# Two chunks' maps as four quarter products in a four-layer graph network

## The chip, the cores and the metric

The kernel runs on one core of one Trainium2 chip. The metric is the device time of one launch in microseconds, lower is better; a kernel's time is the median of its runs. Beside the timed runs there is one profiled execution, from which every duration below comes.

## The reference, cut to what matters

Eight graphs share 2048 nodes with 64 features each. Four layers follow one another, each a LayerNorm, a ReLU, a graph layer and a residual. The change touches layer 2, which takes three steps of the same recurrence:

```python
def _L2_gnn_ref(causal_vars, adj_matrix, intervention_value, W1, b1, W2, b2, intervention_idx):
    v = causal_vars.at[:, intervention_idx].set(intervention_value)
    for _ in range(MAX_STEPS):                       # 3
        effects = jnp.einsum('nm,bmd->bnd', adj_matrix, v)
        h = jnp.concatenate([v, effects], axis=-1)
        h = jax.nn.relu(jnp.einsum('bnk,dk->bnd', h, W1) + b1)
        v = jnp.einsum('bnk,dk->bnd', h, W2) + b2
    return v
...
h = jnp.maximum(_layernorm(x, axis=-1), 0.0)
x = x + _L2_gnn_ref(h, adj, L2_gnn_intervention_value, L2_gnn_W1, L2_gnn_b1, L2_gnn_W2, L2_gnn_b2, 0)
```

Layer 3 takes products of the adjacency with the features twice (Chebyshev terms) and applies a weight of each node's own.

## The kernel before, in words

**Layout.** Two graphs make a pair and stand one above the other on the 128 partitions: partitions 0 to 63 hold the features of graph 0 of the pair, 64 to 127 those of graph 1; nodes run along the free dimension. There are 4 pairs (`p`), and 4 chunks (`c`) of 512 nodes in a pair. A weight of 64x64 that acts on features stands twice on the diagonal of a 128x128 matrix (`W1v`, `Wvc`, `Wec`), and half of such a matrix is zero.

**Layer 2.** `W1` is split into the part for `v` and the part for `effects`. The map by `W2` after a step is folded into the weights of the next one: `Wvc` and `Wec` are those folded matrices, `b1c` and `cb` the folded biases. In steps 1 and 2, `v` therefore holds the ReLU of the step before. For each pair and step the kernel has `y`, the features of all 16 node tiles multiplied by the `effects` weights, nodes on partitions, as a high and a low part in fp32r. For each chunk one PSUM accumulator `acc` (two buffers) takes

- one fp32 product of 128x128 by 128x512, `Wvc` (in step 0 `W1v`) times the chunk of `v` (L2081), and then
- in `spread`, for each of the 16 node tiles `m` two fp32r products, the high and the low part of `y` with the adjacency tile `aT[m]` (L1984 to L1991).

ScalarE writes the ReLU of the accumulator back into the chunk of `v` (L2084). After steps 0 and 1, `carry` makes the chunk's part of the next step's `y`: `moved` multiplies the chunk by `Wec` (four products `py`, one for each node tile), VectorE adds the bias (`yb`, L1952), ScalarE casts the high part (L1954) and VectorE takes the low part (L1955). After step 2, `leave` multiplies by `W2` (`pv`), adds the residual, transposes (`tx`), normalizes for layer 3, and transposes back (`tv`).

**What sets the order.** TensorE's order is that of the program. The chains `carry` and `leave` are Python generators, and a `Weave` with a clock of estimated microseconds slips their pieces in among the products: each `spread` tile counts 0.47, the product by `Wvc` 0.93, and a chain that yields `1.4` gives its next piece once the clock has passed 1.4 after its start. The other engines' order comes from the framework's scheduler, each engine executes in order, and a tile whose memory was used before waits for that use.

**Beside it.** In steps 0 and 1, `raw` loads two blocks of the adjacency a chunk on SP's queue into a tag `x` of two buffers, and `check` (L1927) tests on VectorE that they hold only zeros and ones. At the first pair `weights(1)` loads the weights of layer 3 (`W3f`, two halves on SP, L2062) and the embedding, and `weights(2)` changes `W3f` on VectorE (L2066, L2067). Just before layer 2, layer 1 ends with `e` (L1760) on VectorE and a DMA on GpSimd's queue that adds `e` to memory (L1762).

All matmuls of these layers go through one helper, so they carry the line L734 (transposes L741) in the profile; they are told apart by the tile that they write and by their shapes.

Of the kernel before, what the change touches and what calls it, by code (L numbers as in the profile page):

```python
# [8 lines left out]
FP = mybir.dt.float32  # L9
FR = mybir.dt.float32r  # L10
AF = mybir.ActivationFunctionType
# [5 lines left out]
P = 128  # L17
# [3 lines left out]
NT = N // P  # L21
CW = 512
# [5 lines left out]
def half(b2):  # L28
    return slice(b2 * 64, (b2 + 1) * 64)


def cols(c, w=CW):
    return slice(c * w, (c + 1) * w)
# [602 lines left out]
class Kit:  # L636
# [95 lines left out]
    def mm(self, *args, **kw):  # L732

        one = self.nc.tensor.matmul(*args, **kw)  # L734
        if self.strict:
            self.tc.keep_in_program_order(one)
# [1162 lines left out]
def layers23(self, aT):  # L1899
    kit, x2_dram, x3_dram, out, ctx, fin, v = (  # L1900
        self.kit, self.x2_dram, self.x3_dram, self.out, self.ctx, self.fin, self.v
    )
    tc, nc, t, mm = kit.tc, kit.nc, kit.t, kit.mm
    W1v, W1e, W2, Wvc, Wec, cb = kit.W1v, kit.W1e, kit.W2, kit.Wvc, kit.Wec, kit.cb
    b1, b2c, ivc, b1c = kit.b1, kit.b2c, kit.ivc, kit.b1c
    K3, D3 = 3, 16
    LAST = NCW - 1
    w2 = ctx.enter_context(tc.tile_pool(name="w2f", bufs=1, reuse_waits="tile"))
    sb = ctx.enter_context(tc.tile_pool(name="f_sb", bufs=2, reuse_waits="tile"))
    ps = ctx.enter_context(tc.tile_pool(name="f_ps", bufs=2, space=PSUM, reuse_waits="tile"))  # L1910
    weave = Weave()
# [26 lines left out]
    LENT = (None, None, ("fold", 2), ("pr", 3))  # L1938

    def moved(v, c, W, bias, lent=None):  # L1940

        py = ps.tile([P, 4, P], FP, tag="tp", name="py")
        for k in range(4):
            m = 4 * c + k
            mm(py[:, k, :], v[:, m * P : (m + 1) * P], W, start=True, stop=True)
        return in_parts(py, bias, lent)

    def in_parts(py, bias=None, lent=None):
        hi, lo = parts(lent)
        if bias is not None:  # L1950
            yb = fin.tile([P, 4, P], FP, tag="ca", name="yb")
            nc.vector.tensor_tensor(yb, py, bias[:, None, :].to_broadcast([P, 4, P]), op=OP.add)  # L1952
            py = yb
        nc.scalar.copy(hi, py)  # L1954
        nc.vector.tensor_tensor(lo, py, hi.bitcast(FP), op=OP.subtract)  # L1955
        return hi, lo
# [27 lines left out]
    def spread(acc, y, c, start, ms):  # L1984

        for m in ms:
            weave.until(lambda: y[m // 4] is not None)
            for h, part in enumerate(y[m // 4]):
                mm(acc, part[:, m % 4, :], aT[m][:, cols(c)], start=start, stop=m == NT - 1 and h == 1)
                start = False  # L1990
            weave.passed(0.47)  # L1991

    def load(dst, src, c):
        nc.sync.dma_start(out=dst, in_=src[:, cols(c)])
        return dst

    def chunk_of(src, c):
        return load(fin.tile([P, CW], FP, tag="x", name="xp"), src, c)
# [8 lines left out]
        y[c] = moved(src, k, W1e, None)  # L2007

    def carry(c, step, yn):
        yield 1.4  # L2010
        yn[c] = moved(v, c, Wec, cb, None if step else LENT[c])

    def leave(p, c, xp, yn):

# [40 lines left out]
    y = self.y  # L2055
    W3 = w2.tile([P, K3, D3 * F], FP, name="W3f")
    emb = w2.tile([P, NT, D3], FP, name="embf")

    def weights(step):
        if step == 1:  # L2060
            for h in range(2):
                nc.sync.dma_start(out=W3[half(h)], in_=t["L3_gnn_weight"])  # L2062
            nc.sync.dma_start(out=emb, in_=t["L3_gnn_embedding"].rearrange("(t p) d -> p t d", p=P))
            return

        nc.vector.tensor_sub(W3[:, 0, :], W3[:, 0, :], W3[:, 2, :])  # L2066
        nc.vector.tensor_scalar(W3[:, 2, :], W3[:, 2, :], 2.0, None, op0=OP.mult)  # L2067

    every = range(NT)
    for p in range(NP):  # L2070
        for step in range(3):
            yn = [None] * NCW
            if p == 0 and step:
                weights(step)
            for c in range(NCW):
                acc = ps.tile([P, CW], FP, tag="acc", name="acc")
                if step < 2:
                    got = raw(2)
                else:
                    xp = chunk_of(x2_dram[p], c)  # L2080
                mm(acc, Wvc if step else W1v, v[:, cols(c)], start=True, stop=False)  # L2081
                weave.passed(0.93)
                spread(acc, y, c, False, every)
                nc.scalar.activation(v[:, cols(c)], acc, AF.Relu, bias=b1c if step else b1)  # L2084
                if step < 2:
                    check(got)
                weave.start(carry(c, step, yn) if step < 2 else leave(p, c, xp, yn))
            y = yn


        y1 = sb.tile([P, N], FP, tag="y1", name="y1", bufs=1)
        yn, after = [None] * NCW, [None] * NCW

        two = [ps.tile([P, CW], FP, tag="acc", name="acc") for c in range(2)]
        for ms in (range(0, 8), range(8, 12), range(12, NT)):
            for c in range(2):
                spread(two[c], y, c, 0 in ms, ms)
                if NT - 1 in ms:
                    nc.scalar.copy(y1[:, cols(c)], two[c])
                    weave.start(again(y1, c, yn))  # L2100
        for c in range(2, NCW):
            acc = ps.tile([P, CW], FP, tag="acc", name="acc")
            spread(acc, y, c, True, every)
            nc.scalar.copy(y1[:, cols(c)], acc)
            weave.start(again(y1, c, yn))
        xn = None
        for c in range(NCW):
            xr = chunk_of(x3_dram[p], c)
            acc = ps.tile([P, CW], FP, tag="acc", name="acc")
            if xn is not None:  # L2110
                weave.start(enter(c - 1, after, xn, 0.2, ("u0", "u1")))
                if c == LAST:
                    weave.start(enter(c, after, xl, 0.6, ("u0", "u1"), y1))
            spread(acc, yn, c, True, every)
            y2 = fin.tile([P, CW], FP, tag="ca", name="y2")
            nc.scalar.copy(y2, acc)
            if c < LAST and p + 1 < NP:
                xn = chunk_of(x2_dram[p + 1], c)
                if c == LAST - 1:
                    xl = load(y1[:, cols(0)], x2_dram[p + 1], LAST)  # L2120
            for k in range(4):
                i = 4 * c + k
                ns, ks = slice(i * P, (i + 1) * P), slice(k * P, (k + 1) * P)
                pr = []
                for w in range(2):
                    u = [ps.tile([P, 8, F], FP, tag=f"u{h}", name=f"u{h}") for h in range(2)]
                    for kk, src in enumerate((v[:, ns], y1[:, ns], y2[:, ks])):
                        for h in range(2):

                            mm(  # L2130
                                u[h].rearrange("p d o -> p (d o)"), src[half(h), :], W3[half(h), kk, cols(w)],
                                start=kk == 0, stop=kk == 2,
                            )
                    for h in range(2):
                        a = sb.tile([P, 8, F], FP, tag="pr", name="pr", bufs=3)
                        nc.vector.tensor_tensor(  # L2136
                            a, u[h], emb[:, i, 8 * w : 8 * w + 8, None].to_broadcast([P, 8, F]), op=OP.mult
                        )
                        if w:
                            nc.vector.tensor_add(pr[h], pr[h], a)  # L2140
                        else:
                            pr.append(a)
                    weave.passed(2.8)
                fold = sb.tile([P, 2, 4, F], FP, tag="fold", name="fold")
                ot = sb.tile([P, 2, F], FP, tag="ot", name="ot", bufs=1)
                for h in range(2):
                    nc.vector.tensor_add(fold[:, h], pr[h][:, 0:4, :], pr[h][:, 4:8, :])  # L2147
                nc.gpsimd.tensor_add(fold[:, :, 0:2, :], fold[:, :, 0:2, :], fold[:, :, 2:4, :])  # L2148
                nc.gpsimd.tensor_add(ot, fold[:, :, 0, :], fold[:, :, 1, :])
                nc.gpsimd.tensor_add(ot, ot, xr[:, ks].rearrange("p (h f) -> p h f", h=2))  # L2150
                nc.sync.dma_start(
                    out=out[2 * p : 2 * p + 2, ns, :].rearrange("h p f -> p h f"), in_=ot
                )
        if p + 1 < NP:
            weave.until(lambda: None not in after)
            nc.scalar.copy(v[:, cols(LAST)], y1[:, cols(1)])
        y = after
# [103 lines left out]
```

## Time and profile before

| | us |
|---|---|
| median of 3 runs | 1951.25 (1949.47 to 1952.59) |
| profiled execution | 1953.49, span 1951.7 |
| TensorE busy | 1888.2 |
| layers 2 and 3 of one pair, from one to the next (1138.93 to 1408.64) | 269.7 |
| TensorE's granted clock, mean | 0.989 |

The profile covers one execution. "Busy" is the time in which an engine has at least one instruction under way; PE is TensorE's matmuls, PEld its weight loads, DVE VectorE, ACT ScalarE, POOL GpSimd, and SPq or POOLq an engine's own queue of DMA issues. A group of instructions reads: line, engine, operation, output <- inputs, shape, count | busy us, mean ns of one | idle time before. An fp32 product makes two records, an fp32r product one. The duration of a matmul record includes the pipeline's latency, so the pace of a stream is read from the distance between starts and not from the mean. In the timeline each row is start us, length us, engine, line, operation, and in brackets the idle time before it and what ended it. The share of the chain by line, second row, shows what of TensorE's work carries the time:

```profile
PE acc L734 33%; PE u L734 13%; PE o L734 6%; PE dn L734 3%; PE py L734 3%; PE pgs L734 2%; PE acc L1058 2%; PE pd L734 2%; PE var L734 1%; PE mean L734 1%; DMA iv<-ind_dram 1%; DMA at<-in_adjT 1%; DVE pt L1733 1%; PE pv L734 1%; PE pm L734 1%
```

`acc` of L734 is the work of layers 2 and 3 described above, `u` the per-node weights of layer 3, `o` and `dn` the attention of layer 1.

### The profile page before, as it was taken

The page shows a single profiled execution, that of the slowest core. Times are in us where ns is not written, and L with a number is a line of the kernel's source. Part 1 is how long each engine was busy: PE and PEld are TensorE (multiplying, and loading weights), DVE is VectorE, ACT ScalarE, POOL GpSimd, SP SyncE. Part 2 cuts the span into 40 slices and gives each one's busy share as a digit, 9 for nine tenths or more (in the row PEclk, how much of TensorE's full clock was granted, in tenths as well). Part 3 has the DMA queues.
Part 4 walks back from the last instruction along what each step waited for, and adds up shares of the span by engine and source line. Part 5 has one row for each costly group of instructions (what it writes and reads, how often), then busy time and mean ns, then how long its engine had stood idle before and what let it go on. Part 6 is the DMA issues. An engine that isn't in the chain of part 4 may idle for free.

```text
span 1951.7 us, 23508 instructions
## 1 busy us (share of the span) xinstructions
PE 1888.2 (97%) x9060; PEld 1141.7 (58%) x9060; DVE 1191.2 (61%) x1917; ACT 437.4 (22%) x923; POOL 310.3 (16%) x435
## 2 busy tenths in 40 slices
PE   7999999888999999999999999999999999999997
PEld 6877767423323232247775567765577755677653
DVE  8676499667899998973327652346723266523465
ACT  6322355564212110111220101301112201012100
POOL 4111187311000000000002110111200022101122
PEclk9999899999999999999999999999999999999999
DMA  7656385374121212214200112101022011121000
GB/s 211 174 177 180 121 249 148 97 200 82 41 62 40 61 43 55 65 23 116 60 22 25 30 43 71 49 10 30 24 74 59 22 25 30 43 71 49 5 19 12
DMA packets 86363, 142.43 MB, mean 73 GB/s; under 512 B 33801, under 2 KB 34057, under 8 KB 83569
## 3 DMA queue, kind: packets, MB, share of 16 engines
q1 hardware_dynamic: 65200, 83.86, 14.8%
q0 software_dynamic: 21040, 56.98, 12.0%
q8 instruction: 73, 1.20, 0.3%
q14 instruction: 50, 0.40, 0.1%
HBM read 106.85 MB, written 37.09 MB: 74 GB/s over the span
## 4 chain that ended last, share of the span: by engine, by line
PE 74%; issue 14%; DVE 4%; DMA 3%; POOL 3%; ACT 1%; SPq 0%; POOLq 0%; DVEq 0%; ACTq 0%
PE acc L734 33%; PE u L734 13%; PE o L734 6%; PE dn L734 3%; PE py L734 3%; PE pgs L734 2%; PE acc L1058 2%; PE pd L734 2%; PE var L734 1%; PE mean L734 1%; DMA iv<-ind_dram 1%; DMA at<-in_adjT 1%; DVE pt L1733 1%; PE pv L734 1%; PE pm L734 1%
## 5 line engine op out<-in xcount | busy, mean ns | idle before, releaser
L734 PE MATMUL acc<-aT,parts 128*128 128x512 f32 x1664 | 462.0, 421 | 0.0
L734 PEld LDWEIGHTS acc<-aT,parts 128*128 128x128 f32 x1664 | 306.6, 188 | 111.8 <-issue 51.3
L734 PE MATMUL u<-W3f,y 64*128 64x512 f32 x1024 | 243.2, 589 | 0.0
L1733 DVE SCALAR_TENSOR_TENSOR pt<-R,wd,aT 128x1024 f32<-128x1024 f32 x192 | 236.1, 1279 | 9.7 <-DMA R<-r_dram 4.7
L734 PE MATMUL o<-pt,hS 128*64 128x512 f32 x1024 | 237.2, 599 | 0.8 <-DVE pt L1733 0.6
L2136 DVE TENSOR_TENSOR pr<-u,embf 128x512 f32<-128x512 f32 x256 | 170.7, 688 | 110.2 <-PE u L734 103.2
L734 PEld LDWEIGHTS u<-W3f,y 64*128 64x128 f32 x1024 | 102.3, 187 | 118.0 <-issue 118.0
L734 PEld LDWEIGHTS o<-pt,hS 128*64 128x64 f32 x1024 | 68.4, 136 | 159.9 <-issue 149.2
L734 PE MATMUL u<-W3f,v 64*128 64x512 f32 x512 | 135.0, 596 | 0.0
L2148 POOL TENSOR_TENSOR fold<-fold 128x256 f32<-128x256 f32 x64 | 47.7, 746 | 498.4 <-DVE fold L2147 498.4
L734 PE MATMUL dn<-pt,vd 128*32 128x512 f32 x1024 | 123.1, 598 | 0.0
L1952 DVE TENSOR_TENSOR yb<-py,cb_f 128x512 f32<-128x512 f32 x32 | 22.1, 691 | 161.3 <-PE py L734 161.3
L1058 PE MATMUL acc<-at,Y 128*128 128x512 f32 x384 | 104.7, 415 | 0.0
L734 PE MATMUL acc<-aTl,parts 128*128 128x512 f32 x384 | 98.8, 395 | 0.0
L2140 DVE TENSOR_TENSOR pr<-pr 128x512 f32<-128x512 f32 x128 | 88.2, 689 | 2.2
L2042 POOL TENSOR_TENSOR bq<-bq,xp 128x512 f32<-128x512 f32 x16 | 20.6, 1289 | 430.1 <-ACT xp L2025 430.1
L1733 DVE SCALAR_TENSOR_TENSOR pt<-R,wd,aTl 128x1024 f32<-128x1024 f32 x64 | 79.8, 1282 | 12.4 <-PE dn L734 8.2
L734 PEld LDWEIGHTS u<-W3f,v 64*128 64x128 f32 x512 | 57.3, 186 | 49.6 <-issue 36.1
L734 PEld LDWEIGHTS acc<-aTl,parts 128*128 128x128 f32 x384 | 71.4, 188 | 16.2
L1058 PEld LDWEIGHTS acc<-at,Y 128*128 128x128 f32 x384 | 70.7, 194 | 14.6 <-issue 1.3
L734 PEld LDWEIGHTS dn<-pt,vd 128*32 128x32 f32 x1024 | 26.9, 108 | 80.9 <-issue 75.9
L1966 DVE TENSOR_TENSOR parts<-tp,parts 128x512 fp32r<-128x512 f32 x16 | 11.1, 692 | 85.7 <-ACT parts L1965 85.7
(354 smaller groups left out, 2688.6 us busy)
## 6 DMA issues: line engine op xcount, KB each, us to landing
at<-in_adjT POOLq DMA_DIRECT2D x32, 512.0 KB, 5.5
raw<-in_adjT SPq DMA_DIRECT2D x64, 256.0 KB, 3.4
aT<-in_adjT POOLq DMA_DIRECT2D x12, 1024.0 KB, 6.2
xp<-xd SPq DMA_DIRECT2D x45, 256.0 KB, 3.0
R<-r_dram SPq DMA_DIRECT2D x14, 512.0 KB, 3.8
hlo<-lo_dram POOLq DMA_DIRECT2D x18, 235.1 KB, 3.7
hhi<-hi_dram POOLq DMA_DIRECT2D x18, 235.1 KB, 3.4
hi_dram<-hi SPq DMA_DIRECT2D x16, 264.0 KB, 3.4
```

Source lines behind the costliest of these rows:

```text
L734: one = self.nc.tensor.matmul(*args, **kw)
L1058: mm(acc[p], Y[h][:, m, p, :], at[:, k, :], start=m + h == 0, stop=m == NT - 1 and h == 1)
L1733: nc.vector.scalar_tensor_tensor(pt, R[b2], wd[:, m, b2 : b2 + 1], aT[m][:, s].bitcast(FP), op0=OP.max, op1=OP.mult)
L1952: nc.vector.tensor_tensor(yb, py, bias[:, None, :].to_broadcast([P, 4, P]), op=OP.add)
L1966: nc.vector.tensor_tensor(lo, tp, hi.bitcast(FP), op=OP.subtract)
L2042: nc.gpsimd.tensor_add(bq, bq, xp)
L2136: nc.vector.tensor_tensor(a, u[h], emb[:, i, 8 * w : 8 * w + 8, None].to_broadcast([P, 8, F]), op=OP.mult)
L2140: nc.vector.tensor_add(pr[h], pr[h], a)
L2148: nc.gpsimd.tensor_add(fold[:, :, 0:2, :], fold[:, :, 0:2, :], fold[:, :, 2:4, :])
```

## The change

In steps 1 and 2 the two products by `Wvc` of an even chunk and of the odd chunk after it are no longer made as two products of 128x128. Both accumulators are allocated at the even chunk, the graph sum of its first 8 node tiles is done, and then `quarters` issues four products of 64x64 by 512: for each of the two chunks `d` and each partition half `h`, the 64x64 weight times half `h` of the chunk. For the even chunk (`d == 0`) the result goes to the same half of its accumulator, for the odd chunk to the other half, so that the four products lie on the four quarters of the array. For this the odd chunks of `v` are kept with the two graphs swapped: their ReLU in steps 0 and 1 is two activations of 64 partitions that write into the other half, and `carry` uses for them a matrix `Wxc` with the two blocks of `Wec` off the diagonal, which puts the result back in place. `carry`'s delay for odd chunks goes from 1.4 to 1.9. The product by `W1v` in step 0 remains as it was.

```diff
+    def quarters(accs, W, c):
+
+        for d in range(2):
+            for h in range(2):
+                mm(accs[d][half(h ^ d)], W[half(h), half(h)], v[half(h), cols(c + d)], start=d == 1, stop=False)
+        weave.passed(0.6)
...
     def carry(c, step, yn):
-        yield 1.4
-        yn[c] = moved(v, c, Wec, cb, None if step else LENT[c])
+        yield 1.9 if c % 2 else 1.4
+        yn[c] = moved(v, c, Wxc if c % 2 else Wec, cb, None if step else LENT[c])
...
     emb = w2.tile([P, NT, D3], FP, name="embf")
+    Wxc = w2.tile([P, P], FP, name="Wxc")
+    nc.vector.memset(Wxc, 0.0)
+    for h in range(2):
+        nc.vector.tensor_copy(Wxc[half(h), half(1 - h)], Wec[half(h), half(h)])
...
             for c in range(NCW):
-                acc = ps.tile([P, CW], FP, tag="acc", name="acc")
+                if step == 0 or c % 2 == 0:
+                    accs = [ps.tile([P, CW], FP, tag="acc", name="acc") for d in range(2 if step else 1)]
+                acc = accs[c % 2 if step else 0]
                 if step < 2:
                     got = raw(2)
                 else:
                     xp = chunk_of(x2_dram[p], c)
-                mm(acc, Wvc if step else W1v, v[:, cols(c)], start=True, stop=False)
-                weave.passed(0.93)
-                spread(acc, y, c, False, every)
-                nc.scalar.activation(v[:, cols(c)], acc, AF.Relu, bias=b1c if step else b1)
+                if step == 0:
+                    mm(acc, W1v, v[:, cols(c)], start=True, stop=False)
+                    weave.passed(0.93)
+                    spread(acc, y, c, False, every)
+                elif c % 2 == 0:
+                    spread(acc, y, c, True, range(0, 8))
+                    quarters(accs, Wvc, c)
+                    spread(acc, y, c, False, range(8, NT))
+                else:
+                    spread(acc, y, c, False, every)
+                b = b1c if step else b1
+                if step < 2 and c % 2:
+                    for h in range(2):
+                        nc.scalar.activation(v[half(1 - h), cols(c)], acc[half(h)], AF.Relu, bias=b[half(h)])
+                else:
+                    nc.scalar.activation(v[:, cols(c)], acc, AF.Relu, bias=b)
```

## The prediction

> **What bounds the kernel now.** I read the page first: busy shares, the 40 slices, the chain that ended last.
>
> ```profile
> PE 1888.2 (97%) x9060; PEld 1141.7 (58%) x9060; DVE 1191.2 (61%) x1917; ACT 437.4 (22%) x923; POOL 310.3 (16%) x435
> ...
> PE   7999999888999999999999999999999999999997
> ...
> PE 74%; issue 14%; DVE 4%; DMA 3%; POOL 3%; ACT 1%; SPq 0%; POOLq 0%; DVEq 0%; ACTq 0%
> ```
>
> TensorE is busy 97% of the span and over 90% in every slice of the last two layers (slice 18 on); no other engine comes near. Next the groups of instructions by line, with shapes kept apart, for the products that the change replaces, and the chain piece by piece (start, length, work, records) for what they cost:
>
> ```profile
> L734 PE MATMUL acc<-v,Wvc_f 128*128 128x512 f32 x64 | 32.6, 591 | 0.0
> ```
>
> ```profile
> 1158.86 8.32 PE acc L734 x34
> 1168.08 8.32 PE acc L734 x34
> ...
> 1270.16 7.48 PE acc L734 x32
> ...
> 1323.08 20.81 PE u L734 x96
> ```
>
> The 64 records are 32 products: an fp32 product is two records. A chunk of layer 2 is one such product and 32 records of the graph sum, 8.32 us; the same 32 records without it, in layer 3, take 7.48 us, so a product costs 0.84. Single records of the trace say it closer: its two records start 0.429 us apart, each graph-sum record 0.233 after the last, and product to next real start is 0.858. Chunks follow at 1168.08 - 1158.86 = 9.22 us, which is 8.32 and the map `py` (8 records, 0.89): TensorE never waits there. A microsecond taken off TensorE in these steps comes off the end.
>
> How part-array products run is seen in layer 1 (timeline of TensorE: start, length, line, operation, shape, records):
>
> ```profile
> 735.18 1.92 PE L734 MATMUL dn<-pt,vd 128*32 128x512 f32 x16
> 737.03 3.65 PE L734 MATMUL o<-pt,hS 128*64 128x512 f32 x16
> ```
>
> `dn` puts 8 products into 1.85 us (next start minus own start): four column tiles, with different moving data, start 7 ns apart and share each 0.429 us round. `o` does so with two column tiles. `u` above, with two row tiles, does 24 pairs in 20.81 us, 0.867 a pair. So row tiles overlap and column tiles overlap; both at once, as four 64x64 quarters, no row shows.
>
> **What the Trainium skill says.** TensorEngine Tiling (Array Packing), section Key Properties: changing the tiling mode drains the array. The trace agrees, with a price. Into `u`, the last graph-sum record starts 0.323 us ahead where 0.233 is usual, and the first round takes 0.533 instead of 0.429: 0.19 us. Out of `u`, 0.519 instead of 0.422 and then 0.338 instead of 0.233: 0.20 us. In front of `o`, with its 64-column weights, the first round is 0.480, so the way in is nearer 0.14.
> TensorE: Matmul & The Clock Gate, section Measured speedup vs the span model: row and column packing compose, a pack costing one product and about 4 ns a tile. The trace shows 7 ns for column tiles and nothing for the composition.
> TensorEngine Tiling, Gotcha 1, says that row tiles cannot use one PSUM bank at the same time; here the two graphs' products for one chunk go from different row halves into one bank. PSUM — Partial Sum Buffer, section PSUM bank collisions raise a hardware error, narrows it: an error for one bank and one 32-partition quadrant, no arbitration or stall. These write different partition halves, so I expect neither; no run here shows it.
>
> **The change part by part.**
> *Removed:* the 32 full products, 32 x 0.858 = 27.5 us.
> *Added:* 16 groups of four quarters (4 pairs x 2 steps x 2 even chunks). Each: two rounds 2 x 0.429 = 0.86, stagger 3 x 0.007 = 0.02, the way in 0.16 (between 0.14 and 0.19), the way out 0.20. Sum 1.24; 16 x 1.24 = 19.8 us. Lower bound, both switches free: 0.88 a group, 14.1 in all. Upper: quarters in turn, below.
> TensorE alone: 27.5 - 19.8 = 7.7 us less.
> *The halves of the odd relus:* 16 relus become two activations of 64 partitions. No row has one; half of 0.69 is the lower bound, 0.69 each the upper, which I take, as the number of columns is unchanged. In steady state the relu starts 0.26 us after the chunk's end, so both are done at 1.64. The map waiting for them is moved back (due 1.9, not 1.4): in the changed order it follows five tiles in steps one and two, 5 x 0.467 = 2.33 us, and in step zero W1v and three tiles, 2.26. Margin 0.6, cost nothing; without it 0.69 each, 11 us.
> *That map's result, y[3],* is read at tile 12 of the next step. Before, it is ready 3.2 us after the map starts: now at 2.33 + 3.2 = 5.5, against 12 x 0.467 + 0.89 + 1.24 = 7.7. Free.
> *Both accumulators at once:* the second is first written at tile 8, 3.7 us after the odd chunk whose relu frees it: free. In step two the relu now stands ahead of Ln and Exp in ScalarE's order; their result goes to a transpose which has about 1.5 us to spare. Free.
> *Wxc.* One memset and two copies on VectorE, and not free. In the changed order the memset stands behind the last `e` of layer 1 and ahead of the first adjacency checks `raw`, and it waits for the DMA that reads `e`, whose memory Wxc takes. What stands there (timeline, then the landing of L1762, then of `raw`, from the page):
>
> ```profile
> 876.55 0.68 DVE L1927 SCALAR_TENSOR_TENSOR raw<-raw 128x512 f32<-128x512 f32 x1
> ...
> 876.93 0.93 POOL L1762 DMA_DIRECT2D xd<-e  x1 [8.33 <-DVE e L1760]
> ...
> 877.27 0.94 SPq L1920 DMA_DIRECT2D raw<-in_adjT  x2
> ...
> 878.37 1.14 SPq L2062 DMA_DIRECT2D W3f<-in_L_gnn_weight  x2
> ...
> 892.99 1.23 DVE L2066 TENSOR_TENSOR W3f<-W3f 128x1024 f32<-128x1024 f32 x1 [6.74 <-DMA W3f<-in_L_gnn_weight]
> ...
> 894.86 0.68 DVE L1952 TENSOR_TENSOR yb<-py,cb_f 128x512 f32<-128x512 f32 x1
> ...
> 895.58 0.62 ACT L1954 CAST parts<-yb 128x512 fp32r<-128x512 f32 x1 [8.47 <-DVE yb L1952]
> ...
> 896.10 0.68 ACT L2084 ACTIVATE v<-acc,b_f 128x512 f32<-128x512 f32 x1
> ...
> 896.84 0.97 PEld L734 LDWEIGHTS py<-Wec_f,v 128*128 128x128 f32 x8 [0.35 <-ACT v L2084]
> ```
>
> ```profile
> DMA to landing us min/median/max: 5.5/5.7/7.6
> ```
>
> ```profile
> raw<-in_adjT SPq DMA_DIRECT2D x64, 256.0 KB, 3.4
> ```
>
> Read it as a chain: the second `raw` pair is issued once the first checks free their buffers, the W3f weights follow on SP, VectorE stops for them at 892.99, and behind it hang yb, cast, the relu of chunk 2 and the map `py`, which already waits 0.35 us. Now the DMA is issued at 876.93 and, being the slowest of its row, lands 7.6 later at 884.5. Memset and copies, by estimate 0.3; two checks 0.61 each, so 886.1. In SP's new order the first W3f half goes ahead of the `raw` pair, but the second behind it, at about 886.8. That pair lands 3.4 later (the row above, issue at 886.3), so 889.7; the half's own packets take 4.5 (half of the 9 us in which both halves move), and VectorE started 1.0 after the last packet: 895.2. Then 1.87 for both W3f operations (892.99 to 894.86), 0.7 yb, 0.7 cast, 0.7 relu: the map starts at 899.2 instead of 896.84, 2.4 us late. Bounds: 0 if the weights still land at 893, 5 if the second half takes its 11 us again. The first map with Wxc also waits some 0.6 us behind a late cast, inside that sum. It happens once; later y are read microseconds after.
>
> *Sum:* -7.7 + 2.4 = -5.3 us. The profiled execution, span 1951.7 in a time of 1953.49, becomes 1948.2; on the median of the runs shown, 1951.25, which lies 2.2 below it, 1946.0.
>
> **The rivals.**
> *The quarters don't overlap four-fold* (slower). For: Gotcha 1, and no 64x64 row in the trace. Against: the row and column evidence and the separate partitions. Two and two, a group is 4 x 0.429 + 0.36 = 2.08 us, 16 x (2.08 - 1.72) = +5.8, with the start +8.2: 1959.4. One after another, 3.79 us: +33.1 and 2.4: 1986.8. It decides from 1.57 us a group, where the 16 x 0.15 still saved only pay the 2.4.
> *The weights land in time,* so nothing is late: 1951.25 - 7.7 = 1943.5. For: the first W3f half now leaves earlier. Against: VectorE stands still for 8 us ahead of the second's release.
> *The gain is eaten:* the start costs 5 us or more and an odd relu runs into its map here and there, 0.2 us over 16 places: -7.7 + 5 + 3 = +0.3, 1951.5. For: py already waits once for a relu. Against: the 0.6 us margins.
> *Switching costs nothing* for so short a group: 27.5 - 14.1 = 13.4 less, 2.4 back: 1940.3. Against: every edge of `u` shows both switches.
>
> **How the numbers follow.** Forecast 0.52, its own range 1944 to 1948.5; weights in time 0.20; gain eaten 0.09; switches free 0.03; quarters not four-fold 0.16. A measurement of this kernel can tell 0.2%, 3.9 us, from no change, that is below 1947.3 or above 1955.2. The forecast lies 1.3 us inside: I give 0.45 of its 0.52 to faster. Faster 0.45 + 0.20 + 0.03 = 0.68; same 0.07 and 0.08 of the third = 0.15; slower 0.16 + 0.01 = 0.17. The range 1941.5 to 1952 takes in forecast, weights in time and gain eaten, with both bounds of the start; it leaves out the slower case and the free switches, 0.19.
>
> **What would show it.** Right: a group `acc<-v,Wvc_f` of 64x512 x128, its records in two rounds 0.43 apart, graph-sum start to graph-sum start over it 1.2 us more than usual; pairs of chunks in steps one and two near 18.0 us instead of 18.4; the memset at about 884.5; one wait of `py` for a relu of 2 to 3 us near 897; no new wait for `py` elsewhere. Wrong: groups of 1.7 us or more, recurring PE waits after odd chunks, or W3f landing by 893 or after 898.

## The result, and the profile after

The changed kernel is faster: the ratio to the kernel before is 0.9964, 95% interval 0.9951 to 0.9977 (medians of 20 runs each, 1948.38 and 1955.46 us). Run a second time beside other kernels, it had 0.9975 (0.9958 to 0.9991). The forecast of 5.3 us less, 0.9973, lies in both intervals. It is read as a difference, because the kernel before stood at 1951.25 us when the forecast was made and at 1955.46 in this comparison. The interval alone spans 5 us, so in what follows a few microseconds are read from the traces, and the ratios only have to agree.

The page of the changed kernel, busy shares and the chain's shares by engine:

```profile
PE 1879.6 (97%) x9124; PEld 1132.5 (58%) x9124; DVE 1190.0 (61%) x1920; ACT 448.9 (23%) x939; POOL 311.2 (16%) x435
...
PE 72%; issue 14%; DMA 4%; DVE 4%; POOL 2%; ACT 2%; SPq 0%; POOLq 0%; DVEq 0%; ACTq 0%
```

TensorE's busy time fell by 8.6 us; it is still busy for 97% of the span and carries most of the chain. ScalarE gained 11.5 us: 16 more activations. DMA has a point more of the chain. The chain piece by piece shows two new transfers in it, 16 us together, at the start of layer 2, where the chain of the kernel before has only TensorE's work:

```profile
876.29 7.88 DMA xd<-e
886.65 8.10 DMA W3f<-in_L_gnn_weight
```

What they hold up, and what it costs, is shown below.

Groups of instructions, the product by `Wvc`:

```profile
L734 PE MATMUL acc<-v,Wvc_f 64*64 64x512 f32 x128 | 17.4, 614 | 0.0
```

Twice as many records as before are busy for 17.4 us instead of 32.6. The timeline of TensorE around the first group (start, length, operation, records):

```profile
909.94 1.65 PE L734 MATMUL acc<-aT,parts 128*128 128x512 f32 x6
911.52 1.09 PE L734 MATMUL acc<-v,Wvc_f 64*64 64x512 f32 x8
912.54 0.50 PE L734 MATMUL acc<-aT,hi 128*128 128x512 f32 x1
912.88 0.39 PE L734 MATMUL acc<-aT,lo 128*128 128x512 f32 x1
```

All eight records of four products stand within 1.09 us, and the switch out is seen in the first distance after them, 0.34 instead of 0.233. In the single records the four products start at 0, 7, 13 and 20 ns, the second round follows 0.48 us after the first, and from the last graph-sum record before the group to the second one after it there are 1.675 us, in 12 of the 16 groups (the other four stand between transposes). Less two usual distances, a group takes 1.208.

The start of layer 2 (timeline, several engines; in brackets the idle time before and what ended it; in this kernel L2066 and L2068 build `Wxc`, L2107 is the relu in halves, L2109 the whole one, L2073 and L2077 are the load and the change of `W3f`):

```profile
876.06 0.50 SPq L2073 DMA_DIRECT2D W3f<-in_L_gnn_weight  x1
...
884.32 0.17 DVE L2066 MEMSET Wxc<- 128x128 f32 x1 [8.33 <-DMA xd<-e]
884.51 0.39 DVE L2068 COPY Wxc<-Wec_f 64x64 f32<-64x64 f32 x2
...
885.67 0.94 SPq L1920 DMA_DIRECT2D raw<-in_adjT  x2
...
886.65 0.49 SPq L2073 DMA_DIRECT2D W3f<-in_L_gnn_weight  x1
...
886.89 0.62 ACT L1954 CAST parts<-yb 128x512 fp32r<-128x512 f32 x1 [9.87 <-DVE yb L1952]
...
888.98 0.97 PEld L734 LDWEIGHTS py<-Wxc,v 128*128 128x128 f32 x8 [1.65 <-ACT v L2107]
...
894.84 1.23 DVE L2077 TENSOR_TENSOR W3f<-W3f 128x1024 f32<-128x1024 f32 x1 [3.47 <-DMA W3f<-in_L_gnn_weight]
...
898.81 0.97 PEld L734 LDWEIGHTS py<-Wec_f,v 128*128 128x128 f32 x8 [1.73 <-ACT v L2109]
```

VectorE stands idle for 8.33 us in front of the memset, until the DMA that reads `e` has landed. The `raw` pair, which went out at 877.27 before the change, goes out at 885.67; the second half of the weights follows at 886.65; VectorE has them at 894.84. Two maps `py` wait for relus that stand behind late casts on ScalarE: the first, 1.65 us, because the `yb` that its cast reads stood behind the memset on VectorE, the second, 1.73 us, because its `yb` stood behind the change of `W3f`. That is the part of the change which costs. `W3f` itself is needed only at the first `u`, at 1021.78, so its place in VectorE's order is a second thing that could be moved; no run here moves it.

To have one measure for all kernels, I take from the starts of the records the time of layer 2 with the first half of layer 3, from a pair's first product by `W1v` to its first `u`. What a kernel does in every pair is in pairs 2 to 4; the first pair has the start of layer 2 in addition.

| kernel | ratio to before (95%) | first pair, us | mean of pairs 2 to 4, us |
|---|---|---|---|
| before | 1 | 153.29 | 153.06 |
| changed | 0.9964 (0.9951 to 0.9977) | 154.08 | 151.06 |
| changed, again | 0.9975 (0.9958 to 0.9991) | 153.78 | 151.04 |
| Wxc built early | 0.9955 (0.9938 to 0.9972) | 151.48 | 151.06 |
| Wxc on GpSimd | 0.9965 (0.9953 to 0.9977) | 151.37 | 151.04 |
| full products | 1.0012 (1.0000 to 1.0025) | 155.81 | 153.12 |
| no swap | 1.0034 (1.0022 to 1.0046) | 154.73 | 154.40 |
| delay 1.4 | 1.0006 (0.9991 to 1.0021) | 155.33 | 152.63 |
| quarters at the chunk's start | one run, 1970.08 us beside 1951.74 | 159.35 | 156.67 |
| step 0 too, Wxc built early | 0.9949 (0.9929 to 0.9969) | 151.41 | see below |

The change saves 2.0 us in each pair, and in the first pair loses 2.8 (2.5 in the second run of it) at the start: over the four pairs 612.5 became 607.3 and, again, 606.9 us. The profiled span fell by 6.8; the rest is not in this measure. The layers before layer 2, which the change does not touch, ended anywhere between 867.6 and 872.5 us in the ten profiles, so a microsecond or two there means nothing.

### The profile page after: what moved, and what is told of

Its sections match the earlier page's. It is cut to its first block, busy times and chain, and to the rows that moved or that the text cites. A ratio compares the mean times of both kernels' runs of the same rounds, so it can differ in the third digit from the quotient of the medians.

```text
span 1944.9 us, 23640 instructions
## 1 busy us (share of the span) xinstructions
PE 1879.6 (97%) x9124; PEld 1132.5 (58%) x9124; DVE 1190.0 (61%) x1920; ACT 448.9 (23%) x939; POOL 311.2 (16%) x435
## 3 DMA queue, kind: packets, MB, share of 16 engines
q8 instruction: 74, 1.21, 0.3%
## 4 chain that ended last, share of the span: by engine, by line
PE 72%; issue 14%; DMA 4%; DVE 4%; POOL 2%; ACT 2%; SPq 0%; POOLq 0%; DVEq 0%; ACTq 0%
PE acc L734 31%; PE u L734 13%; PE o L734 5%; PE dn L734 3%; PE py L734 3%; PE pd L734 2%; PE pgs L734 2%; PE acc L1058 2%; PE var L734 1%; PE mean L734 1%; DMA at<-in_adjT 1%; DMA iv<-ind_dram 1%; DVE pt L1733 1%; PE pm L734 1%; PE ph L734 1%
## 5 line engine op out<-in xcount | busy, mean ns | idle before, releaser
L734 PE MATMUL acc<-aT,parts 128*128 128x512 f32 x1664 | 448.4, 413 | 0.0
```

## The experiments

### Full products in the same place

```diff
     def quarters(accs, W, c):
-        for d in range(2):
-            for h in range(2):
-                mm(accs[d][half(h ^ d)], W[half(h), half(h)], v[half(h), cols(c + d)], start=d == 1, stop=False)
+        mm(accs[0], W, v[:, cols(c)], start=False, stop=False)
+        mm(accs[1], Wvx, v[:, cols(c + 1)], start=True, stop=False)
```

`Wvx` holds the blocks of `Wvc` off the diagonal; VectorE builds it in the first pair.

> The changed kernel with everything kept (both accumulators at the even chunk, products after tile 8, odd chunks swapped, relu halves, Wxc) but the four quarters made as two full products, the odd chunk's with Wvc's blocks off the diagonal. Theory (all of the gain is the array shared by four): 2 x 0.858 = 1.72 us where a group took 1.21, 16 x 0.508 = 8.1 us above the changed kernel and 2.8 above the kernel before, ratio 1.0014. Rival (part of the gain is the new place or the two accumulators, fewer waits at chunk edges): less than 5 us above the changed kernel, and below the kernel before.

Measured: 1.0012 (1.0000 to 1.0025), and 153.12 us a pair, within 0.06 of the kernel before. The timeline of TensorE in this kernel:

```profile
915.84 1.02 PE L734 MATMUL acc<-v,Wvc_f 128*128 128x512 f32 x2
916.70 1.02 PE L734 MATMUL acc<-v,Wvx 128*128 128x512 f32 x2
917.15 0.79 PE L734 MATMUL acc<-aT,hi 128*128 128x512 f32 x1
917.78 0.40 PE L734 MATMUL acc<-aT,lo 128*128 128x512 f32 x1
```

The two products start 0.86 us apart. From the last graph-sum record before them to the second after them there are 2.174 us; less two usual distances that is 1.71, two whole products and nothing for a switch. The new place, the two open accumulators, the swap and the relu halves together neither gain nor cost anything in a pair. The first pair carries 155.81 - 153.12 = 2.7 us more than the others (0.2 in the kernel before), the price of the start, since Wxc is still built there, and Wvx after it. The whole gain is the shared array, and the rival is out: 2.06 us a pair over four groups is 0.515 a group.

### The quarters without the swap

```diff
-                mm(accs[d][half(h ^ d)], W[half(h), half(h)], v[half(h), cols(c + d)], start=d == 1, stop=False)
+                mm(accs[d][half(h)], W[half(h), half(h)], v[half(h), cols(c + d)], start=d == 1, stop=False)
...
-        yn[c] = moved(v, c, Wxc if c % 2 else Wec, cb, None if step else LENT[c])
+        yn[c] = moved(v, c, Wec, cb, None if step else LENT[c])
...
-                if step < 2 and c % 2:
-                    for h in range(2):
-                        nc.scalar.activation(v[half(1 - h), cols(c)], acc[half(h)], AF.Relu, bias=b[half(h)])
-                else:
-                    nc.scalar.activation(v[:, cols(c)], acc, AF.Relu, bias=b)
+                nc.scalar.activation(v[:, cols(c)], acc, AF.Relu, bias=b)
```

Wxc and its memset are gone too.

> The changed kernel without the swap: all chunks of v keep their order, relu whole, no Wxc; the four 64x64 products then use only the two quarters on the diagonal, twice each, and each pair on the diagonal still writes one PSUM bank. Theory: four rounds of 0.429 and 0.35 for the two switches, 2.07 us a group where two full products took 1.72; 16 x 0.36 = 5.7 us above the kernel before, ratio 1.003, with no wait at the start. Rival (two row halves cannot use one bank together, and only the order across banks saved the changed kernel): 8 rounds, 3.8 us a group, 33 us above, ratio 1.017.

Measured: 1.0034 (1.0022 to 1.0046), 154.40 us a pair. The timeline of TensorE:

```profile
908.75 1.93 PE L734 MATMUL acc<-v,Wvc_f 64*64 64x512 f32 x8
910.62 0.50 PE L734 MATMUL acc<-aT,hi 128*128 128x512 f32 x1
```

The same eight records need 1.93 us instead of 1.09, two rounds more. A pair is 1.34 us longer than before the change, 0.335 a group: 1.716 + 0.335 = 2.05, expected 2.07. Small products alone are a loss; it is the swap that puts the odd chunk on the two idle quarters. The run settles the bank question as well: two row halves that write different partition halves of one PSUM bank run side by side, otherwise this would have been 3.8 us a group. This is the forecast's slower rival, two and two, made real: as a mechanism it exists, and its price, 2.08 there, was right within 0.03 us a group. The first pair is only 0.3 us longer than the others, as there is no Wxc to build.

### Wxc out of VectorE's way, in two manners

First, Wxc in the lasting pool, built in layer 0 behind Wec:

```diff
     def layer2_weights(self, pool, ps, W2n):
...
             nc.vector.tensor_copy(dst, pw)
+        nc.vector.memset(self.Wxc, 0.0)
+        for h in range(2):
+            nc.vector.tensor_copy(self.Wxc[half(h), half(1 - h)], self.Wec[half(h), half(h)])
...
-    Wxc = w2.tile([P, P], FP, name="Wxc")
-    nc.vector.memset(Wxc, 0.0)
-    for h in range(2):
-        nc.vector.tensor_copy(Wxc[half(h), half(1 - h)], Wec[half(h), half(h)])
+    Wxc = kit.Wxc
```

> The changed kernel with Wxc in the lasting pool and built beside Wec, in layer 0, so that no memory of layer 1 is waited for. Theory (the memset's wait holds up VectorE and, through the raw pair and the second W3f half, the map of chunk 2): W3f starts on VectorE near 893 instead of 894.8, the map of chunk 2 waits 0.35 us as before the change instead of 1.73, and the time is 2.9 us below the changed kernel, 8.1 us below the kernel before (16 x 0.508), ratio near 0.996. Rival (the weights come late whatever VectorE does, since they share queues with the DMA of e): the map waits over 1.2 us as in the changed kernel, no gain over it.

Measured: 0.9955 (0.9938 to 0.9972); the first pair 151.48 us instead of 154.08, the others unchanged. The timeline at the start of layer 2 (the helper is L737 in this kernel):

```profile
878.33 1.14 SPq L2073 DMA_DIRECT2D W3f<-in_L_gnn_weight  x2
...
892.94 1.23 DVE L2077 TENSOR_TENSOR W3f<-W3f 128x1024 f32<-128x1024 f32 x1 [6.76 <-DMA W3f<-in_L_gnn_weight]
...
896.91 0.97 PEld L737 LDWEIGHTS py<-Wec_f,v 128*128 128x128 f32 x8 [0.59 <-ACT v L2109]
```

Both halves of the weights go out together again, they are used at 892.94, and the map of chunk 2 starts at 896.91 instead of 898.81, after a wait of 0.59 us (0.35 expected, 1.73 in the changed kernel). The chain still runs through `W3f` here (13.98 us), so a place in the chain is not yet a cost. The 2.6 us of the first pair stand for the theory's 2.9; the ratio, 0.0009 lower than the changed kernel's, agrees but could not have shown it alone.

Second, Wxc in the same memory, so with the same wait, but on GpSimd:

```diff
-    nc.vector.memset(Wxc, 0.0)
+    nc.gpsimd.memset(Wxc, 0.0)
     for h in range(2):
-        nc.vector.tensor_copy(Wxc[half(h), half(1 - h)], Wec[half(h), half(h)])
+        nc.gpsimd.tensor_copy(Wxc[half(h), half(1 - h)], Wec[half(h), half(h)])
```

> The changed kernel with Wxc in the same memory, but its memset and copies on GpSimd. Theory (what costs is VectorE standing still behind the memset's wait, not that Wxc is late): Wxc still waits for the DMA of e until about 884.4 and is ready before the first map that needs it at 888; W3f starts on VectorE near 893, the map of chunk 2 waits under 0.7 us, and layer 2 of the first pair (its first product to the first u) takes 151.5 us as with Wxc built early, not 154.1. Rival (the late Wxc or the shared queues cost it): 153 us or more.

Measured: 0.9965 (0.9953 to 0.9977), first pair 151.37 us. The timeline:

```profile
885.40 0.20 POOL L2066 MEMSET Wxc<- 128x128 f32 x1 [6.89 <-DMA xd<-e]
885.67 0.50 POOL L2068 COPY Wxc<-Wec_f 64x64 f32<-64x64 f32 x2
...
888.96 1.10 PEld L734 LDWEIGHTS py<-Wxc,v 128*128 128x128 f32 x8
...
893.76 1.23 DVE L2077 TENSOR_TENSOR W3f<-W3f 128x1024 f32<-128x1024 f32 x1 [6.78 <-DMA W3f<-in_L_gnn_weight]
...
897.73 0.97 PEld L734 LDWEIGHTS py<-Wec_f,v 128*128 128x128 f32 x8 [0.53 <-ACT v L2109]
```

The memset still waits for the DMA, here until 885.40 (layer 2 began 1.6 us later in this profile than in that of the changed kernel), and Wxc is ready 2.8 us before its first use. The cost is gone all the same. So it was never that Wxc came late: it was what stood queued behind the memset on VectorE. The total doesn't show the 2.7 us, 0.9965 against 0.9964 and 0.9975: they are below what these runs tell apart, and the statement rests on the traces, those of the two kernels without the stop (151.48 and 151.37 us) and the two of the changed kernel (154.08 and 153.78).

### The odd chunks' map as early as before

```diff
-        yield 1.9 if c % 2 else 1.4
+        yield 1.4
```

> The changed kernel with carry's delay for odd chunks back at 1.4, so that the map with Wxc comes two tiles earlier. Theory (the later place is needed because the two relu halves take 1.4 us): the map starts 1.40 us after the chunk's end (1.33 behind W1v) while the second half ends at 1.67, so 16 waits of about 0.3 us, 4 to 5 us above the changed kernel. Rival (the place makes no difference, the halves are covered): equal to the changed kernel, no wait of py for the relu except at the start.

Measured: 1.0006 (0.9991 to 1.0021), 152.63 us a pair. Groups of weight loads, the map by Wxc, in this kernel; then in the changed kernel:

```profile
L734 PEld LDWEIGHTS py<-Wxc,v 128*128 128x128 f32 x128 | 15.5, 191 | 10.8 <-ACT v L2107 10.8
```

```profile
L734 PEld LDWEIGHTS py<-Wxc,v 128*128 128x128 f32 x128 | 16.7, 191 | 3.0 <-ACT v L2107 1.6
```

The idle time before the map grew from 3.0 to 10.8 us, all of it for the relu; that includes time in which TensorE still had a product under way. On the path it is 1.57 us a pair, 0.39 for each of four odd chunks, somewhat over the 0.3 expected. Over the four pairs 6 us are lost against the changed kernel, and 613.2 us is even 0.7 more than before the change: without the half microsecond of delay nothing of the net gain is left.

### The quarters at the start of the even chunk

```diff
-                    spread(acc, y, c, True, range(0, 8))
-                    quarters(accs, Wvc, c)
-                    spread(acc, y, c, False, range(8, NT))
+                    quarters(accs, Wvc, c)
+                    spread(acc, y, c, False, every)
```

In `quarters`, `start=True` takes the place of `start=d == 1`, because the products now open both accumulators.

> The changed kernel with the four quarters put at the start of the even chunk, where Wvc's product stood, instead of after tile 8. Theory (the second accumulator comes free only with the relu of the chunk just ended, 1.67 us after its end in halves and 0.95 whole, so the place after tile 8 is part of the change): the even chunk's two quarters run, the odd chunk's two wait; a group takes 1.5 us more behind a relu in halves (3 of 4 groups of a pair) and 0.9 more behind a whole one, 5.4 us a pair, some 21 us above the changed kernel. Rival (the place does not matter): no more than 3 us above it.

Measured in one run: 1970.08 us beside 1951.74 of the kernel before; 156.67 us a pair, 5.6 more than the changed kernel (5.4 expected). The timeline of TensorE:

```profile
907.72 1.08 PE L734 MATMUL acc<-v,Wvc_f 64*64 64x512 f32 x4
909.27 1.08 PE L734 MATMUL acc<-v,Wvc_f 64*64 64x512 f32 x4 [0.47 <-ACT v L2106]
```

The group falls in two: the even chunk's pair runs, the odd chunk's waits for the second accumulator until the relu halves of the chunk just ended have read it. Three of a pair's four groups do so and take 1.6 us more than in the changed kernel (1.5 expected). In the fourth, behind a whole relu, the second pack starts 0.85 us after the first, the length of its two rounds. The group takes 2.04 us there instead of 1.208, 0.8 more (0.9 expected): the price of two half-filled packs without a wait. The place after tile 8 gives nothing by itself, as the full products showed, but the quarters need it.

### A version beyond both

Wxc built early, and the quarters in step 0 too, in all pairs but the first (`p` 1 to 3, the pairs 2 to 4 of the table). For this the odd chunks enter swapped:

```diff
-                if step == 0 or c % 2 == 0:
-                    accs = [ps.tile([P, CW], FP, tag="acc", name="acc") for d in range(2 if step else 1)]
-                acc = accs[c % 2 if step else 0]
+                first = step == 0 and p == 0
+                if first or c % 2 == 0:
+                    accs = [ps.tile([P, CW], FP, tag="acc", name="acc") for d in range(1 if first else 2)]
+                acc = accs[0 if first else c % 2]
...
-                if step == 0:
+                if first:
...
-                    quarters(accs, Wvc, c)
+                    quarters(accs, Wvc if step else W1v, c)
...
+        if swap:
+            nc.vector.scalar_tensor_tensor(xc, xc, 0.0, dst, op0=OP.max, op1=OP.mult)
+            for h in range(2):
+                nc.scalar.copy(dst[half(1 - h)], xc[half(h)])
...
-            nc.scalar.copy(v[:, cols(LAST)], y1[:, cols(1)])
+            for h in range(2):
+                nc.scalar.copy(v[half(1 - h), cols(LAST)], y1[half(h), cols(1)])
```

> Wxc built early, and the quarters also in step 0 of pairs 1 to 3 (with W1v; the odd chunks of v are written swapped when they enter, one by two ScalarE copies in place of nothing, one by two half copies in place of one). Theory (a group is worth 0.508 us wherever TensorE is the bound): 6 more groups, 3.0 us below the kernel with Wxc built early, layer 2 of pairs 1 to 3 at 150.0 us instead of 151.05; ratio to the kernel before 0.994. Rival (the swapped chunks come later into step 0, whose first maps now wait): no gain, 151 us or more.

Measured: 0.9949 (0.9929 to 0.9969), the lowest of all. The start of step 0 has no product there any more, so the measure of the table doesn't fit; from the first `u` of one pair to that of the next (chain of this kernel):

```profile
1019.27 20.81 PE u L737 x96
...
1285.93 20.81 PE u L737 x96
```

266.66 us, where Wxc built early has 267.64 (1019.94 to 1287.58) and the kernel before 270.06 (1021.96 to 1292.02). Two more groups save 0.98, 0.49 each; from the first `u` of the first pair to that of the last it is 3.0 us, as expected. That it beats the kernel with Wxc built early is shown by this distance, not by the ratios, whose intervals overlap.

## Why the prediction was right

*TensorE as the bound, so that its microseconds come off the end:* right. 16 groups at 1.208 instead of 1.716 make 8.1 us, and pairs 2 to 4 each lost 2.0. One reading of the page was off: the last slice stands at 7, not over 90%; nothing in the sum rests on it.

*The group of 1.24 us:* measured 1.208. The terms, read off the records: two rounds 0.858, stagger 0.020, the way out 0.195, near the 0.20 seen at `u`, the way in 0.136 and not 0.16. The way in came out at what the row of `o` had suggested; the forecast had taken a middle between it and `u`. TensorE's part is then 8.1 against 7.7.

*Four quarters in the array at once,* which no row of the kernel before showed: shown, by starts 7 ns apart. The Trainium skill's composition of row and column packing (TensorE: Matmul & The Clock Gate, Measured speedup vs the span model) held here for fp32 quarters, with 7 ns a tile instead of 4. Gotcha 1 (TensorEngine Tiling (Array Packing)), that different row tiles cannot access the same PSUM bank simultaneously, does not hold by the word: two row halves wrote different partition halves of one bank side by side, in the changed kernel and without the swap. That agrees with the narrower statement of PSUM — Partial Sum Buffer, section PSUM bank collisions raise a hardware error, which ties the error to bank and quadrant, though the section also quotes the wider one. No run here puts two row tiles into one quadrant.

*The relu halves:* taken at 0.69 each, the upper bound. Each takes 0.68 in the trace, so halving the partitions saves nothing. Both are free on the path, as forecast, given their delay; the run without the delay shows that the margin was needed.

*y[3], both accumulators, the relu ahead of Ln:* costed at nothing, and the full products show that all of them together cost 0.06 us a pair.

*The start:* the chain was right link by link in its order and causes, and its sizes a little short. Memset predicted 884.5, measured 884.32; the second half of the weights issued 886.8 against 886.65, used 895.2 against 894.84; map of chunk 2 at 899.2 against 898.81. That the times agree so closely is in part luck, as layer 2 began 0.9 us earlier in this profile than before: counted from there each link came 0.5 to 0.75 us later than forecast, and the map is 2.9 us late where 2.4 was expected. Memset and copies took 0.58 us where 0.3 had been estimated, and the DMA of `e` 7.9 instead of 7.6. The forecast also had one wait of 2 to 3 us at the map of chunk 2, with some 0.6 for the first map with Wxc inside it; the trace has 1.65 there and 1.73 at chunk 2. The first pair puts the cost at 2.8 and 2.5.

*The sum:* -7.7 + 2.4 = -5.3 against -8.1 + 2.8 = -5.3 in the terms, and -5.2 and -5.6 in the four pairs. Two errors of 0.4 with opposite signs happened to cancel. The whole runs say -7.0 with an interval from -9.6 to -4.5, which neither confirms nor contradicts it more closely.

*The rivals:* two and two did not happen here, but exists without the swap; weights in time did not happen, and is what the change gives if Wxc is built early; nothing else ate the gain; and switching was not free, 0.33 us a group.

## What to carry to other kernels

A product with a block-diagonal weight uses half the array; four quarter products fill it only if two of them lie off the diagonal. Keeping every second block of data swapped does that: the quarter product puts the block back in order, and the activation after it, split into halves, swaps it again. Here that was free on the path (0.06 us a pair) only because the map behind the two halves could be put off by half a microsecond. Before crediting such a pack, charge the two mode switches (here 0.33 us against 0.5 saved) and make sure that all its inputs and accumulators are free at one moment, for a pack that splits costs more: here 2.04 us instead of 1.21 before any wait, and 2.8 with it. And a one-time setup of a small constant is not free by being small: ask whose memory it takes, what that use still waits for, and what is queued behind it on the same engine.

## What the runs showed of the hardware that I had not expected

Nothing contradicted the forecast in kind. Three sizes are worth keeping from these traces: going into quarters with 64-column weights costs 0.136 us and coming back to 128 columns 0.195; an activation of 64 partitions by 512 takes 0.68 us, as one of 128 does (0.69); and building the same 128x128 matrix took GpSimd 0.8 us where VectorE took 0.6.
